# Two 3x3 convolutions of a basic block, four output rows at a time from six row combinations

## The chip, the cores and the metric

The kernel runs on one core of a Trainium2 chip. The metric is the device time of one execution in microseconds (us). All data is fp32. The engines are named as the profile names them: PE is TensorE (PEld its weight loads), DVE is VectorE, ACT is ScalarE, POOL is GpSimd, SP is SyncE, whose queue issues most DMAs. Each engine works through its own queue in order; semaphores order the engines among each other.

## What is computed

The input is a batch of 2 images with 128 channels of 128 x 128 points. Four layers follow each other: a convolution with a small state-space model on top, a density gate on windows, a second layer like the first, and a basic block. Only the last is touched by the change:

```python
def _L3_conv_ref(x, w1, gamma1, beta1, w2, gamma2, beta2):
    w1b = w1 + lax.stop_gradient(jnp.sign(w1) - w1)
    w2b = w2 + lax.stop_gradient(jnp.sign(w2) - w2)
    out = jax.nn.relu(_batchnorm(_conv3x3(x, w1b), gamma1, beta1))
    out = _batchnorm(_conv3x3(out, w2b), gamma2, beta2)
    out = out + x
    return jax.nn.relu(out)
```

Both convolutions have 128 input and 128 output channels, 3 x 3 taps and a border of zeros. The batch norms take mean and variance over both images, so a convolution must be complete before its norm can be applied. The input `x` of the block is itself the end of the second layer: silu of a normalised `y`, plus that layer's input.

## The kernel before, in words

`_program` runs the four layers one after the other. The basic block is `_basic_block` (line 820). Channels lie on the 128 partitions. An image is cut into bands of 8 rows (`BAND`), so there are 32 bands over both images, listed in `bands`. The result of a convolution stays in SBUF as `Y`, both images whole.

**Fewer products.** A convolution of 3 rows is not done tap by tap. For each pair of output rows, four combinations of four input rows are formed (`combine`, lines 874 to 881: row 0 minus row 2, row 1 plus row 2, row 2 minus row 1, row 1 minus row 3), the weights are combined in the same way beforehand (lines 838 to 853), and the four products are put together to two output rows. A band of 8 rows has 4 pairs, so each product is a matmul over 4 x 128 = 512 columns; with the three horizontal taps that is 12 matmuls a band in place of 18.

**Weights.** For each of the two weight sets the sign is taken on ACT (line 841), two DVE operations form w + (sign(w) - w) (lines 842 and 843), and DVE builds the four combined sets `u` (lines 848 to 852). The temporary tiles come from the buffers of `comb`, of which there are two.

**The loop.** `convolve` writes the order of every engine out by hand (`manual_schedule` for PE, ACT, DVE, POOL and SP): within it each engine's queue holds the instructions in exactly the order in which the Python code issues them. In round k it calls `load(k+3)`, the step `make(k+2)`, `combine(k+1)` and `conv(k)`:

- `load` (first convolution only): SP issues the DMAs of 10 rows of `y` (line 940) and of the residual `xs` (line 942).
- `make` is `residual` in the first convolution: ACT does the silu in place (line 948), POOL adds the residual (line 949), SP writes the rows to DRAM as `x3` (line 950). In the second it is `normalised`: POOL copies two rows from the band before (line 961), ACT applies norm and relu to rows of `Y` (line 963).
- `combine`: POOL, four instructions of 520 elements a partition (line 880), into a `comb` tile.
- `conv`: PE, 12 matmuls (line 887) into four banks of PSUM (tile `m`, two buffers); ACT copies one product to SBUF (line 895); DVE does four additions of 512 elements (lines 898 to 901), each with one operand in PSUM; two `bn_stats` (line 903).

Three tiles of 10 rows (`room`) hold the bands in turn. After a convolution `affine` (line 908) turns the statistics into scale and shift.

**The output stage** (lines 969 to 977) loads `x3` back, scales, adds, applies relu and stores; its tiles are in turn the two `xs` and the `comb` buffers.

Of the kernel before, what the change touches and what calls it, by code (L numbers as in the profile page):

```python
# [24 lines left out]
F32 = mybir.dt.float32  # L25
U8 = mybir.dt.uint8
AF = mybir.ActivationFunctionType
ALU = mybir.AluOpType
# [3 lines left out]
P = 128  # L32
# [10 lines left out]
BAND = 8  # L43
# [775 lines left out]

def _basic_block(tc, src, y, norm, x3, w1, w2, bn, out, B, H):  # L820

# [3 lines left out]
    nc = tc.nc  # L825
    pairs = BAND // 2
    with tc.tile_pool(name="bb", bufs=1) as cp, tc.tile_pool(name="bband", bufs=2) as bp, tc.tile_pool(
        name="ps_c", bufs=2, space=PSUM
    ) as pp:

        def combined():
            return bp.tile([P, 4, pairs, P + 2], F32, tag="comb", name="comb")

        bnc = cp.tile([P, 4], F32, tag="bnc", name="bnc")
        nc.sync.dma_start(out=bnc, in_=bn)
        ws = []
        for n, wd in enumerate((w1, w2)):
            room = [combined().rearrange("p a b c -> p (a b c)")[:, : 9 * P] for _ in range(2)]
            wt, sg = room
            nc.sync.dma_start(out=wt, in_=wd)  # L840
            nc.scalar.activation(sg, wt, AF.Sign)
            nc.vector.tensor_tensor(sg, sg, wt, ALU.subtract)
            nc.vector.tensor_tensor(wt, wt, sg, ALU.add)

            u = cp.tile([P, 4, 3, P], F32, tag=f"u{n}", name=f"u{n}")
            g = wt.rearrange("p (k t c) -> p k t c", k=3, t=3)
            half = sg.rearrange("p (k t c) -> p k t c", k=3, t=3)
            nc.vector.tensor_copy(u[:, 0:4:3], g[:, 0:3:2])
            nc.vector.tensor_tensor(half[:, 0], g[:, 0], g[:, 2], ALU.add)
            nc.vector.tensor_tensor(u[:, 1], half[:, 0], g[:, 1], ALU.add)  # L850
            nc.vector.tensor_tensor(u[:, 2], half[:, 0], g[:, 1], ALU.subtract)
            nc.vector.tensor_scalar_mul(u[:, 1:3], u[:, 1:3], 0.5)
            ws.append(u)
        Y = cp.tile([P, B, H, P], F32, tag="Y", name="Y")

# [17 lines left out]

        def combine(k):

            xb = span(k)[0]
            v = combined()
            d = [xb[:, n : n + BAND - 1 : 2, :] for n in range(4)]
            for i, (m, n, op) in enumerate(((0, 2, ALU.subtract), (1, 2, ALU.add), (2, 1, ALU.subtract), (1, 3, ALU.subtract))):
                nc.gpsimd.tensor_tensor(v[:, i], d[m], d[n], op)  # L880
            return v

        def conv(u, v, b, r0, stats):
            m = pp.tile([P, 4, pairs, P], F32, tag="m", name="m")
            for i in (1, 2, 0, 3):
                for kw in range(3):
                    nc.tensor.matmul(  # L887
                        m[:, i],
                        lhsT=u[:, i, kw, :],
                        rhs=v[:, i, :, kw : kw + P],  # L890
                        start=(kw == 0),
                        stop=(kw == 2),
                    )
            m1 = bp.tile([P, pairs, P], F32, tag="m1", name="m1")
            nc.scalar.copy(m1, m[:, 1])  # L895
            rows = Y[:, b, r0 : r0 + BAND, :]
            y0, y1 = rows[:, 0:BAND:2, :], rows[:, 1:BAND:2, :]
            nc.vector.tensor_tensor(y0, m1, m[:, 2], ALU.add)  # L898
            nc.vector.tensor_tensor(y1, m1, m[:, 2], ALU.subtract)
            nc.vector.tensor_tensor(y0, y0, m[:, 0], ALU.add)  # L900
            nc.vector.tensor_tensor(y1, y1, m[:, 3], ALU.subtract)
            for n in range(BAND // ROWS):
                nc.vector.bn_stats(
                    stats[:, (b * H + r0) // ROWS + n, :],
                    rows[:, n * ROWS : (n + 1) * ROWS, :].rearrange("p r w -> p (r w)"),
                )
# [9 lines left out]

        def convolve(u, load, make, n):

            stats = cp.tile([P, B * H // ROWS, 6], F32, tag="st", name="st")
            v = {}  # L920
            E = mybir.EngineType
            with tc.manual_schedule(engines={E.PE, E.Activation, E.DVE, E.Pool, E.SP}):
                for k in range(-3, len(bands)):
                    for ahead, f in ((3, load), (2, make)):
                        if 0 <= k + ahead < len(bands):
                            f(k + ahead)
                    if 0 <= k + 1 < len(bands):
                        v[k + 1] = combine(k + 1)
                    if k >= 0:
                        conv(u, v.pop(k), *bands[k], stats)  # L930
            return affine(stats, n)
# [19 lines left out]

        s1, t1 = convolve(ws[0], load, residual, 0)

# [12 lines left out]

        s2, t2 = convolve(ws[1], lambda k: None, normalised, 1)

# [12 lines left out]
def _program(ctx, tc, d, cols, out):  # L981
# [7 lines left out]
    with tc.tile_pool(name="const", bufs=1) as cp, tc.tile_pool(name="wts", bufs=1) as wp:  # L989
# [24 lines left out]
        with tc.tile_pool(name="ps_n", bufs=1, space=PSUM) as pp:  # L1014
            norm = [_norm(nc, npool, pp, w, con, stats, b) for b in range(B)]
    _basic_block(tc, x2, y, norm, x3, d["L3_w1"], d["L3_w2"], d["L3_bn"], out, B, H)

# [42 lines left out]
```

## Time and profile before

| quantity | us |
|---|---|
| median of 3 runs | 7720.45 |
| lowest, highest | 7717.87, 7742.86 |
| profiled execution, its own time | 7727.12 |
| span of the profiled execution | 7725.3 |
| basic block, first weight load to end | 6898.7 to 7725.3 |
| first convolution, first combination to last statistics | 6929.43 to 7268.34 |
| second convolution, the same | 7274.15 to 7612.91 |

The profile shows one execution. A page or an answer of it lists instructions by line, engine, operation and tile, as `out<-in`, with sizes as partitions x elements. In a timeline the first number is the start and the second the duration, both in us; what stands in brackets at the end is how long the engine had been idle before and what ended that. In the groups, `x1536 | 663.6, 595` means 1536 instructions, 663.6 us in which at least one of them ran, 595 ns the mean of one; then the idle time before them. TensorE's granted clock is given as a share of full speed.

### The profile page before, as it was taken

What the parts mean: (1) busy time and instruction counts of PE and PEld (TensorE: products, weight loads), DVE (VectorE), ACT (ScalarE), POOL (GpSimd) and SP (SyncE); (2) the same over time, 40 slices, a digit from 0 to 9 for tenths busy, and PEclk for the clock granted to TensorE, in tenths of its full rate; (3) what the DMA queues carried; (4) which work ended last, traced back from release to release, by engine and by line L of the source; (5) the groups of instructions that cost most, each with busy time, mean ns of one, the idle gap of its engine ahead of it and who ended that gap; (6) DMA issues with size and microseconds to landing.
All of it is one profiled execution on the core that took longest, in us unless ns stands there. A gap on an engine that the chain in (4) does not pass through costs nothing.

```text
span 7725.3 us, 87235 instructions
## 1 busy us (share of the span) xinstructions
PE 6471.5 (84%) x29648; PEld 2190.2 (28%) x29648; DVE 6761.0 (88%) x6304; ACT 4280.1 (55%) x4877; POOL 5630.1 (73%) x1879
## 2 busy tenths in 40 slices
PE   7888888888888888767888888888888888869993
PEld 2222222222222222243222222222222222224441
DVE  6999999999999999966999999999999999983333
ACT  5665666566666666554566656566666566631112
POOL 5777877887877778743787777787777887867541
PEclk8999999999999999877999999999999999979997
DMA  7999999999999999944999999999999999975204
GB/s 205 252 250 245 252 248 246 252 252 247 249 252 250 249 252 253 242 183 149 248 248 250 251 243 251 251 250 253 255 249 244 254 250 247 251 196 177 87 0 169
DMA packets 573438, 1767.29 MB, mean 229 GB/s; under 512 B 85536, under 2 KB 239680, under 8 KB 458176
## 3 DMA queue, kind: packets, MB, share of 16 engines
q1 hardware_dynamic: 568384, 1744.92, 86.4%
q10 hardware_dynamic: 4608, 16.78, 0.5%
q8 instruction: 236, 3.87, 0.2%
q14 instruction: 210, 1.72, 0.1%
HBM read 1551.65 MB, written 209.72 MB: 228 GB/s over the span
## 4 chain that ended last, share of the span: by engine, by line
DVE 37%; DMA 28%; PE 20%; issue 6%; ACT 4%; POOL 3%; SPq 2%; POOLq 0%; DVEq 0%; ACTq 0%
DMA bcr<-sb 21%; DVE set L472 12%; DVE h L477 11%; DVE r L473 10%; PE m L887 9%; DMA ur<-su 3%; POOL h L445 3%; PE set L454 2%; PE one L350 2%; ACT set L463 2%; PE ys L492 1%; PE one L400 1%; DVE v L505 1%; PE ys L483 1%; DMA sb<-bc 1%
## 5 line engine op out<-in xcount | busy, mean ns | idle before, releaser
L445 POOL TENSOR_TENSOR h<-ur,bcr 128x2048 f32<-128x2048 f32 x896 | 4060.8, 4539 | 1291.1 <-DMA bcr<-sb 1038.1
L472 DVE TENSOR_TENSOR set<-set,h 128x1024 f32<-128x1024 f32 x1792 | 2193.5, 1224 | 275.1 <-ACT set L463 170.4
L473 DVE TENSOR_TENSOR r<-set,bcr 128x1024 f32<-128x1024 f32 x1792 | 2194.5, 1225 | 61.5
L463 ACT ACTIVATE set<-set 128x1024 f32<-128x1024 f32 x1792 | 1745.2, 1006 | 844.2 <-PE set L454 833.2
L477 DVE TENSOR_TENSOR h<-set,h 128x1024 f32<-128x1024 f32 x1536 | 1865.9, 1215 | 25.0 <-POOL h L445 24.8
L454 PE MATMUL set<-dt,rep 32*128 32x512 f32 x7168 | 1396.1, 675 | 100.9 <-DVE h L477 94.8
L492 PE MATMUL ys<-r,ct 128*32 128x512 f32 x7168 | 1168.2, 635 | 32.7 <-DVE r L473 32.7
L323 PE MATMUL one<-band,conv 128*128 128x512 f32 x2304 | 1082.9, 606 | 22.6 <-DMA band<-in_x_dram 12.0
L400 PE MATMUL one<-xc,keep 128*64 128x512 f32 x1008 | 318.9, 715 | 462.9 <-ACT xc L357 355.7
L887 PE MATMUL m<-comb,u 128*128 128x512 f32 x1536 | 663.6, 595 | 39.0 <-POOL comb L880 39.0
L454 PEld LDWEIGHTS set<-dt,rep 32*128 32x128 f32 x7168 | 403.2, 193 | 992.5 <-issue 463.7
L323 PEld LDWEIGHTS one<-band,conv 128*128 128x128 f32 x2304 | 407.1, 189 | 669.1 <-issue 596.6
L483 PE MATMUL ys<-t,ct 128*128 128x512 f32 x512 | 327.9, 727 | 251.9 <-DVE v L505 250.3
L352 ACT ACTIVATE xc<-one,keep 128x512 f32<-128x512 f32 x252 | 173.3, 688 | 516.9 <-PE one L350 512.1
L492 PEld LDWEIGHTS ys<-r,ct 128*32 128x32 f32 x7168 | 180.9, 112 | 926.8 <-issue 764.3
L898 DVE TENSOR_TENSOR Y<-m,m 128x512 f32<-128x512 f32 x64 | 44.0, 688 | 435.8 <-ACT m L895 435.8
L880 POOL TENSOR_TENSOR comb<-band 128x520 f32<-128x520 f32 x256 | 298.5, 1198 | 161.7 <-PE m L887 160.1
L887 PEld LDWEIGHTS m<-comb,u 128*128 128x128 f32 x1536 | 291.7, 190 | 410.2 <-issue 363.3
L420 PE MATMUL one<-prod,ct 128*128 128x512 f32 x504 | 282.1, 642 | 118.0 <-POOL prod L412 89.9
L374 POOL TENSOR_TENSOR u<-dt,xc 128x1024 f32<-128x1024 f32 x128 | 303.0, 2367 | 89.7 <-ACT dt L368 89.3
L895 ACT COPY m<-m 128x512 f32<-128x512 f32 x64 | 37.5, 586 | 556.6 <-issue 474.7
L350 PE MATMUL one<-y,w_in 128*128 128x512 f32 x504 | 344.2, 772 | 1.8 <-ACT xc L352 1.8
(144 smaller groups left out, 6292.1 us busy)
## 6 DMA issues: line engine op xcount, KB each, us to landing
ur<-su SPq DMA_DIRECT2D x896, 896.0 KB, 11.6
bcr<-sb SPq DMA_DIRECT2D x896, 448.0 KB, 11.8
ur<-su SPq DMA_DIRECT2D x896, 128.0 KB, 11.2
su<-u SPq DMA_DIRECT2D x1024, 64.0 KB, 3.1
sb<-bc SPq DMA_DIRECT2D x256, 224.0 KB, 2.7
bcr<-sb SPq DMA_DIRECT2D x896, 64.0 KB, 11.1
y<-o SPq DMA_DIRECT2D x128, 256.0 KB, 9.4
band<-in_x_dram SPq DMA_DIRECT2D x28, 640.0 KB, 10.9
```

Source lines behind the costliest of these rows:

```text
L323: nc.tensor.matmul(py.rearrange("p (r w) -> p r w", r=ROWS), lhsT=w["conv"][:, tap, :], rhs=xb[:, r + kh : r + kh + ROWS, kw : kw + P], st ...
L350: nc.tensor.matmul(p, lhsT=w[("in", "z")[i]][:, g, :], rhs=s["y"], start=True, stop=True)
L400: nc.tensor.matmul(p[g * NQ * DS : (g + 1) * NQ * DS, :], lhsT=w[("xb", "xcm")[i]], rhs=s["xc"][:, g, :], start=True, stop=True,)
L445: nc.gpsimd.tensor_tensor(b, s["ur", t], s["bc", t][:, 0].unsqueeze(1).to_broadcast([P, NJ, NS]), ALU.mult)
L454: nc.tensor.matmul(a[j // 2][:, j % 2, :], lhsT=w["rep"][r, q, :], rhs=s["dt"][r, g, :], start=True, stop=True, tile_position=(r.start, 0),)
L463: nc.scalar.activation(x, x, AF.Exp)
L472: nc.vector.tensor_tensor(pt, pt, s["h", t - 1][:, js, :], ALU.mult)
L473: nc.vector.tensor_tensor(s["r", t][:, js, :], pt, s["bc", t - 1][:, 1].unsqueeze(1).to_broadcast([P, 2, NS]), ALU.mult)
L477: nc.vector.tensor_tensor(s["h", t][:, js, :], pt, s["h", t][:, js, :], ALU.add)
L483: nc.tensor.matmul(s["ys", g], lhsT=con["ident"], rhs=s["t1"][:, g, :], start=True, stop=False)
L492: nc.tensor.matmul(s["ys", g][a : a + NQ * DJ, :], lhsT=red[:, q, :], rhs=r[:, j, :], start=False, stop=(q == NQ - 1), tile_position=(0, a),)
L887: nc.tensor.matmul(m[:, i], lhsT=u[:, i, kw, :], rhs=v[:, i, :, kw : kw + P], start=(kw == 0), stop=(kw == 2),)
```

## The change

The convolutions are done four output rows at a time from six combinations of six input rows, with weights combined accordingly. Of a band of 8 rows there are now two groups of four (`fours`), so each product has 2 x 128 = 256 columns, and there are six products of three taps: 18 matmuls of 256 columns a band.

The combinations have factors other than 1 and are made in two pieces: `edges` (four DVE `scalar_tensor_tensor` of 260 elements and three POOL `tensor_tensor` of 520, 520 and 260) and `rest_of` (three more DVE operations of 260, in place). `products` is the matmuls alone; `m` takes three banks and keeps two buffers. `conv` copies one bank of two products to SBUF (`c`), forms sums and differences of the products, those of one pair in SBUF (`sd1`) and those of the other in PSUM (`sd2`), and writes `Y` with five more operations.

The pieces of a band are issued one to four rounds apart: in round k, `rest_of(k+1)`, `products(k)`, `conv(k-1)`, `load(k+4)`, `make(k+3)`, `edges(k+2)`. `comb` has three buffers of 6 x 2 x 130 elements in place of two of 4 x 4 x 130.

The six weight sets take more room, so there is one `u`. The second convolution's weights are prepared at the start in a part of `Y` that isn't in use yet, stored to DRAM (`later`) and loaded into `u` between the convolutions.

```diff
         def combined():
-            return bp.tile([P, 4, pairs, P + 2], F32, tag="comb", name="comb")
+            return bp.tile([P, 6, fours, P + 2], F32, tag="comb", name="comb", bufs=3)
...
+            nc.vector.tensor_scalar_mul(x[:, 0], g[:, 0], 0.25)
+            nc.vector.tensor_copy(x[:, 5], g[:, 2])
+            nc.vector.tensor_tensor(even, g[:, 0], g[:, 2], ALU.add)
+            nc.vector.tensor_tensor(x[:, 3], even, g[:, 1], ALU.add)
+            nc.vector.tensor_tensor(x[:, 2], even, g[:, 1], ALU.subtract)
+            nc.vector.tensor_scalar_mul(x[:, 2:4], x[:, 2:4], -1.0 / 6.0)
+            flat = [y.rearrange("p t c -> p (t c)") for y in (even, odd, g[:, 0], g[:, 1], g[:, 2], x[:, 1], x[:, 4])]
+            nc.vector.scalar_tensor_tensor(flat[0], flat[4], 4.0, flat[2], ALU.mult, ALU.add)
+            nc.vector.scalar_tensor_tensor(flat[5], flat[3], 2.0, flat[0], ALU.mult, ALU.add)
+            nc.vector.scalar_tensor_tensor(flat[6], flat[3], -2.0, flat[0], ALU.mult, ALU.add)
+            nc.vector.tensor_scalar_mul(x[:, 1:5:3], x[:, 1:5:3], 1.0 / 24.0)
+        later = scratch.tile([P, 18 * P], F32, tag="later", name="later", bufs=1)
+        nc.sync.dma_start(out=later, in_=spare.rearrange("p a t c -> p (a t c)"))
...
-        def combine(k):
+        def edges(k):
 
             xb = span(k)[0]
             v = combined()
-            d = [xb[:, n : n + BAND - 1 : 2, :] for n in range(4)]
-            for i, (m, n, op) in enumerate(((0, 2, ALU.subtract), (1, 2, ALU.add), (2, 1, ALU.subtract), (1, 3, ALU.subtract))):
-                nc.gpsimd.tensor_tensor(v[:, i], d[m], d[n], op)
+            low, high = [xb[:, n : n + BAND, :].rearrange("p (i n) w -> p n i w", n=4) for n in (0, 2)]
+            for n, at in enumerate((0, 3, 2, 5)):
+                nc.vector.scalar_tensor_tensor(v[:, at], low[:, n], -4.0, high[:, n], ALU.mult, ALU.add)
+            nc.gpsimd.tensor_tensor(v[:, 1:5:3], high[:, 1:3], low[:, 1:3], ALU.subtract)
+            nc.gpsimd.tensor_tensor(v[:, 0:6:5], v[:, 2:6:3], v[:, 0:4:3], ALU.subtract)
+            nc.gpsimd.tensor_tensor(v[:, 3], v[:, 2], v[:, 3], ALU.add)
             return v
 
-        def conv(u, v, b, r0, stats):
-            m = pp.tile([P, 4, pairs, P], F32, tag="m", name="m")
-            for i in (1, 2, 0, 3):
+        def rest_of(v):
+            x = [v[:, n].rearrange("p i w -> p (i w)") for n in range(6)]
+            nc.vector.scalar_tensor_tensor(x[4], x[1], -2.0, x[4], ALU.mult, ALU.add)
+            nc.vector.scalar_tensor_tensor(x[1], x[1], 4.0, x[4], ALU.mult, ALU.add)
+            nc.vector.scalar_tensor_tensor(x[2], x[2], 2.0, x[3], ALU.mult, ALU.subtract)
+
+        def products(v):
+
+            m = pp.tile([P, 3, 2, fours, P], F32, tag="m", name="m")
+            for n, i in enumerate((2, 4, 3, 1, 0, 5)):
                 for kw in range(3):
                     nc.tensor.matmul(
-                        m[:, i],
+                        m[:, n // 2, n % 2],
...
+            return m
+
+        def conv(m, b, r0, stats):
+            c = bp.tile([P, 2, fours, P], F32, tag="c", name="c")
+            nc.scalar.copy(c, m[:, 0])
+            sd1 = bp.tile([P, 2, fours, P], F32, tag="sd", name="sd", bufs=1)
+            sd2 = pp.tile([P, 2, fours, P], F32, tag="sd", name="sd")
+            for n, sd in enumerate((sd1, sd2)):
+                nc.vector.tensor_tensor(sd[:, 0], m[:, 1, n], c[:, n], ALU.add)
+                nc.vector.tensor_tensor(sd[:, 1], m[:, 1, n], c[:, n], ALU.subtract)
             rows = Y[:, b, r0 : r0 + BAND, :]
-            y0, y1 = rows[:, 0:BAND:2, :], rows[:, 1:BAND:2, :]
-            nc.vector.tensor_tensor(y0, m1, m[:, 2], ALU.add)
-            nc.vector.tensor_tensor(y1, m1, m[:, 2], ALU.subtract)
-            nc.vector.tensor_tensor(y0, y0, m[:, 0], ALU.add)
-            nc.vector.tensor_tensor(y1, y1, m[:, 3], ALU.subtract)
+            y = rows.rearrange("p (i n) w -> p n i w", n=4)
+            (s1, d1), (s2, d2) = [(sd[:, 0], sd[:, 1]) for sd in (sd1, sd2)]
+            nc.vector.tensor_tensor(y[:, 0:4:3], m[:, 2], sd1, ALU.add)
+            nc.vector.scalar_tensor_tensor(y[:, 1], d2, 2.0, d1, ALU.mult, ALU.add)
+            nc.vector.scalar_tensor_tensor(y[:, 2], s2, 4.0, s1, ALU.mult, ALU.add)
+            nc.vector.tensor_tensor(y[:, 0], s2, y[:, 0], ALU.add)
+            nc.vector.scalar_tensor_tensor(y[:, 3], d2, 8.0, y[:, 3], ALU.mult, ALU.add)
...
-                for k in range(-3, len(bands)):
-                    for ahead, f in ((3, load), (2, make)):
+                m = {}
+                for k in range(-4, len(bands) + 1):
+                    if 0 <= k + 1 < len(bands):
+                        rest_of(v[k + 1])
+                    if 0 <= k < len(bands):
+                        m[k] = products(v.pop(k))
+                    if k >= 1:
+                        conv(m.pop(k - 1), *bands[k - 1], stats)
+                    for ahead, f in ((4, load), (3, make)):
                         if 0 <= k + ahead < len(bands):
                             f(k + ahead)
-                    if 0 <= k + 1 < len(bands):
-                        v[k + 1] = combine(k + 1)
-                    if k >= 0:
-                        conv(u, v.pop(k), *bands[k], stats)
+                    if 0 <= k + 2 < len(bands):
+                        v[k + 2] = edges(k + 2)
...
+        nc.sync.dma_start(out=u.rearrange("p a t c -> p (a t c)"), in_=later)
+        s2, t2 = convolve(lambda k: None, normalised, 1)
```

## The prediction

> **What bounds the kernel now.** I read first the chain of work that ended last: inside the basic block it is one piece per convolution, TensorE line 887 from 6932.1 to 7263.9 us and again from 7276.6 to 7608.4. Then the busy time by stretch:
>
> ```profile
> 6942.00:7263.00 321.00, 321.00 (x749) 141.37 (x748) 116.80 (x186) 57.10 (x60) 216.10 (x153) 1.00 0.52 164
> 7287.00:7608.00 321.00, 321.00 (x749) 141.18 (x747) 116.77 (x186) 51.13 (x60) 149.69 (x150) 1.00 0.01 2
> ```
>
> Columns after the length: busy us of PE, weight loads, DVE, ACT, POOL, then clock, DMA share, GB/s. TensorE has no idle time at full clock; DVE works 36%, POOL 67% and 47%. So TensorE sets both convolutions. The groups from 6800 us on give prices:
>
> ```profile
> L887 PE MATMUL m<-comb,u 128*128 128x512 f32 x1536 | 663.6, 595 | 39.0 <-POOL comb L880 39.0
> L880 POOL TENSOR_TENSOR comb<-band 128x520 f32<-128x520 f32 x256 | 298.5, 1198 | 161.7 <-PE m L887 160.1 <-DVE u L851 1.6
> ...
> L975 DVE SCALAR_TENSOR_TENSOR comb<-Y,aff_s,comb 128x1024 f32<-128x1024 f32 x16 | 20.5, 1284 | 39.2 <-DMA comb<-x 39.0
> ```
>
> Each fp32 matmul is two records (1536 = 64 bands x 12 x 2). One band in the timeline:
>
> ```profile
> 7150.61 0.59 ACT L895 COPY m<-m 128x512 f32<-128x512 f32 x1 [8.36 <-issue]
> 7151.09 1.46 ACT L948 ACTIVATE band<-band,aff_t,aff_s 128x1280 f32<-128x1280 f32 x1
> 7151.23 0.69 DVE L898 TENSOR_TENSOR Y<-m,m 128x512 f32<-128x512 f32 x1 [6.50 <-ACT m L895]
> 7151.84 0.68 DVE L899 TENSOR_TENSOR Y<-m,m 128x512 f32<-128x512 f32 x1
> 7152.43 0.68 DVE L900 TENSOR_TENSOR Y<-Y,m 128x512 f32<-128x512 f32 x1
> 7152.63 2.68 POOL L949 TENSOR_TENSOR band<-band,xs 128x1280 f32<-128x1280 f32 x1 [3.01 <-ACT band L948]
> 7153.03 0.68 DVE L901 TENSOR_TENSOR Y<-Y,m 128x512 f32<-128x512 f32 x1
> 7153.75 1.29 DVE L903 BATCH_NORM_STATS2 st<-Y 128x6 f32<-128x512 f32 x2
> 7155.27 4.65 POOL L880 TENSOR_TENSOR comb<-band 128x520 f32<-128x520 f32 x4
> ```
>
> The next L895 is at 7160.91: a band lasts 10.30 us. DVE operations of 512 elements start 0.60 apart though each lasts 0.68, except that bn_stats waits for L901's end (0.72). L880 starts every 1.16.
>
> Last, what no steady band shows: DVE operations with two SBUF inputs beside POOL. The weight preparation has them:
>
> ```profile
> 6920.76 2.71 POOL L949 TENSOR_TENSOR band<-band,xs 128x1152 f32<-128x1152 f32 x1 [8.95 <-DMA xs<-x]
> 6921.26 3.43 DVE L843 TENSOR_TENSOR comb<-comb 128x1152 f32<-128x1152 f32 x1
> ...
> 6924.78 3.03 POOL L949 TENSOR_TENSOR band<-band,xs 128x1280 f32<-128x1280 f32 x1 [1.31 <-DMA xs<-x]
> 6925.19 3.03 DVE L849 TENSOR_TENSOR comb<-comb 128x384 f32<-128x384 f32 x1
> ```
>
> Alone, these DVE lines took 1.34 and 0.56 us (first weight set). Here each stood until POOL's instruction ended (6923.47, 6927.81), then ran: ends 1.22 and 0.41 later. And after line 660, with two POOL instructions back to back:
>
> ```profile
> 3509.68 4.68 POOL L662 TENSOR_TENSOR x<-xr,g 128x1024 f32<-128x1024 f32 x2 [4.46 <-ACT g L660]
> 3511.61 0.52 DVE L760 TENSOR_SCALAR e<-e 128x128 f32<-128x128 f32 x1
> 3513.16 1.28 DVE L762 TENSOR_SCALAR e<-e 128x128 f32<-128x128 f32 x1
> ```
>
> L760 got through where the first L662 ended (3512.0); it did not wait for the second. A DVE operation already standing slips between two POOL instructions; one that comes after the second has begun waits it out (L762).
>
> **What the Trainium skill says.** "SBUF — State Buffer", Who interferes with whom: a Vector instruction with two SBUF inputs and a GpSimd instruction that reads SBUF exclude each other for a whole instruction; with one SBUF input it does not contend. The rows above agree, and L898 to L901 (one input in PSUM) keep 0.68 beside L949. "TensorE: Matmul & The Clock Gate", Step-by-step: the next weights load under the running matmul. Agrees: 0.19 us loads under matmuls 0.429 apart. The same page, Part 1: some 3.4 us of idleness halve the clock. After the 12.7 us pause at 7264 the first matmuls stood 0.85 apart for 4 us.
>
> **The change, part by part (per band).**
> TensorE: 18 matmuls of 256 columns for 12 of 512. 24 records in 10.30 us are 0.429 each; half the columns is 0.215, above the 0.19 of a load (line 512 runs 16 records of 128 columns, with loads, in 2.05, 0.13 each). 36 x 0.215 = 7.75 us. Gain alone: 2.55 x 64 = 163 us, if nothing else is late.
>
> DVE: now 4 operations and 2 statistics; then 18. Slope 1.05 ns an element (L842, 1152: 1.36; L849, 384: 0.56), so start to start 256 elements cost 0.60 - 256 x 1.05 = 0.33, 260 cost 0.34. A scalar_tensor_tensor with immediate scalars isn't in the trace; L975, with per-partition scalars, starts every 1.20 against 1.14 for a tensor_tensor of 1024: 0 to 0.065 more; I take 0.03. Names: R1 to R3 are rest_of, S1 to S4 the sums and differences, W1 to W5 the writes to Y, E1 to E4 the edges; P1 to P3 POOL's three in edges.
> S1 to the next edges: S 4 x 0.33 + W1 0.60 + W2 to W4 3 x 0.33 + 0.06 + W5 to its end 0.48 + two statistics 1.21 = 4.7. None has two SBUF inputs (sd2 and m are PSUM).
> E1 to the end of E4: 3 x 0.37 + 0.44 = 1.55.
> Then the place that decides. Order on DVE: E(k+2), at once R(k+1) of the next round, whose operands came from the E and P just before. From E4's end = 0: R1 starts at -0.08 and holds the port to 0.34; P2 (520 elements, needs E4) runs to 1.54; R2 slips in to 1.84; P3 (260; 1.16 - 260 x 2.1 ns = 0.61) to 2.4. R3 needs P3's result. POOL's queue has its next instruction waiting: in the first convolution residual's L949 (operands ready for us: the load is issued a round earlier and lands in 4.5 to 5.6), which begins before R3 has its signal. R3 stands 2.69 to 5.1, and S1 starts at 5.3. In the second the next is L961, 0.40: S1 at 3.0.
> Behind the waiting R3 on DVE stand conv's nine operations, the statistics and the next edges; TensorE waits for R3 (its first product reads that combination) and for W1, which frees m. Nothing else may run in DVE's queue meanwhile.
> load and make move one round further ahead and behind conv: on ACT the copy of m now precedes the silu (both done a round early); on POOL the order residual, then combinations stays; on SP the three DMAs of a band (4.5, 5.6 and 3.2 us to landing) keep their order and have the whole longer round: nothing, and if a load came late, L949 would move behind R3, a gain.
> So a round is 5.3 + 4.7 + 1.55 = **11.55 us** in the first convolution and 3.0 + 4.7 + 1.55 = **9.25** in the second. TensorE's 7.75 (9.8 if 4 us of each round ran at half clock after the 3.8 us pause) lies under both, m being double; ACT (0.59 + 1.46), POOL (5.6) and the DMAs (1.8 MB a round) too. DVE, not TensorE, sets the end.
> Whole convolutions, E1(0) to the last statistics: 1.55 + two rounds without conv + 29 full + (R and conv) + two conv alone. First: 1.55 + 13.7 + 335 + 10 + 9.4 = 370, against 6929.43 to 7268.34 = 339 now: **+31**. Second: 1.55 + 9.1 + 268 + 7.7 + 9.4 = 296 against 7274.15 to 7612.91 = 339: **-43**.
> Setup: some 5 more DVE operations for each weight set, 2.3 us each; the second set no longer waits for a buffer (its load was issued at 6912.45, now with the first). I take +1; -3 to +10, the high end if the store of the second set holds the band loads behind it on SP's queue. The reload of u (1.18 MB; some 8 us from 4.5 for 0.64 MB) starts at the last matmul and is wanted after conv's rest, 5.8 us of affine and normalising, E and R, some 13 us: nothing; uncovered, it would cost 8. The output stage keeps its chain (xs slots): 0, bounds -3 and +3.
> Sum: +31 - 43 + 1 = -11. On the profiled 7727.1 (span 7725.3): 7716; the median is 6.7 lower, so **7709**.
>
> **Rivals.**
> *R3 gets ahead of L949*, if POOL needs a moment to start it: S1 at 2.75 in the first convolution, 2.55 x 32 = 82 less: 7627. For: L760 slipped in. Against: it stood there already, and consecutive L880 overlap by 0.04.
> *No exclusion for this operation*: S1 at 2.25 in both; 3.05 x 32 + 0.75 x 32 = 122 less: 7587. Against: L843, L849.
> *Slower: DVE loses every hand-over.* R2 stands behind P2, P3, the residual or copy and P1 of the next band: S1 at 6.5 and 4.2, 1.2 x 64 = 77 more: 7786. For: POOL's queue is full there. Against: L760. It decides once the two rounds add up to over 21.1 us (I have 20.8): 0.3 us is all that lies between.
>
> **How the numbers follow.** The likeliest case has 0.52; its ends come from the scalar_tensor_tensor price (10 x 0.03 x 62 = 19 down, 10 x 0.035 x 62 = 22 up), setup and output: 7685 to 7744. R3 ahead 0.13, no exclusion 0.06, lost hand-overs 0.20, smaller waits on DVE not counted here (some 7750) 0.09. Range 7625 to 7790: only the 7587 and tails lie outside. A measurement tells 0.3%, 23 us, from no change. Faster: 0.19 + a third of the likeliest case = 0.35; same: the bulk of it = 0.33; slower: 0.29 + the rest = 0.32.
>
> **What would show it.** TensorE idle in every round, records of 256 columns 0.215 apart; rounds of 11.5 and 9.25 us; R3 lasting about 2.9 us in the first convolution and starting just after L949 begins; R2 about 1.5; S and W at 0.33. Wrong if R3 is short, if the rounds of both convolutions are alike, or if TensorE is still without idle time.

## The result, and the profile after

| | before | after |
|---|---|---|
| median of 6 runs each, us | 7726.12 | 7682.67 |
| lowest, highest | 7716.18, 7742.86 | 7668.24, 7699.44 |
| profiled execution, its span | 7725.3 | 7676.1 |

The ratio after to before is 0.9943, 95% interval 0.9924 to 0.9962: 0.57% faster, some 43 us.

The totals also hold the three layers ahead of the basic block, which no kernel here touches. In thirteen profiled executions, one of each kernel of this study, they ended between 6883 and 6923 us. So from here on stages inside the block are compared. Setup runs from the first weight load to the first combination on DVE (on POOL in the kernel before), a convolution from there to its last statistics; the block is the sum of all stages with the 5 to 6 us of affine and normalising between the convolutions.

| stage, us | before | after | difference | predicted |
|---|---|---|---|---|
| setup | 30.7 | 25.6 | -5.1 | +1 |
| first convolution | 338.9 | 360.7 | +21.8 | +31 |
| second convolution | 338.8 | 295.6 | -43.1 | -43 |
| output stage | 112.4 | 101.4 | -11.0 | 0 |
| block | 826.6 | 788.7 | -37.9 | -11 |

Of the two profiled executions' 49 us, 11 lie ahead of the block (6898.75 against 6887.43) and are not the change's. The cut between setup and first convolution is soft: in the kernel after and six of its variants the two from the first weight load to the first R3 (named below) take 33.8 us, while the setup alone varies from 23.1 to 26.7.

The windows of the kernel after, in the middle of each convolution (columns: busy us and number of PE, weight loads, DVE, ACT, POOL; then clock, DMA share, GB/s):

```profile
6950.00:7230.00 280.00, 220.33 (x906) 182.30 (x904) 261.70 (x456) 48.76 (x51) 158.65 (x104) 0.93 0.52 166
7300.00:7530.00 230.00, 208.45 (x943) 176.18 (x942) 211.21 (x458) 44.91 (x52) 101.65 (x103) 1.00 0.00 1
```

Before, PE filled such windows wholly. Now it is busy 79% and 91%, and DVE 93% and 92%: DVE has taken its place. The groups of the kernel after, from 6880 us on:

```profile
L906 PE MATMUL m<-comb,u 128*128 128x256 f32 x2304 | 537.4, 394 | 137.3 <-DVE Y L926 90.8 <-DVE comb L899 46.5
L899 DVE SCALAR_TENSOR_TENSOR comb<-comb 128x260 f32<-128x260 f32 x64 | 97.4, 1521 | 39.5 <-POOL comb L892 39.5
L898 DVE SCALAR_TENSOR_TENSOR comb<-comb 128x260 f32<-128x260 f32 x64 | 88.8, 1388 | 2.2
L897 DVE SCALAR_TENSOR_TENSOR comb<-comb 128x260 f32<-128x260 f32 x64 | 28.0, 438 | 5.0 <-POOL comb L890 5.0
```

PE waited 137 us, all of it for DVE: 46.5 for the first combination of each convolution, 90.8 in the rounds. Three DVE operations of the same form and size, R1 to R3 (lines 897 to 899), took 438, 1388 and 1521 ns on average. A longer operation that has no more to compute is one that stood. One round of the first convolution, in the timeline:

```profile
7100.44 0.42 DVE L897 SCALAR_TENSOR_TENSOR comb<-comb 128x260 f32<-128x260 f32 x1
7100.60 1.42 POOL L891 TENSOR_TENSOR comb<-comb 128x520 f32<-128x520 f32 x1 [4.97 <-DVE comb L889]
7100.90 1.41 DVE L898 SCALAR_TENSOR_TENSOR comb<-comb 128x260 f32<-128x260 f32 x1
7102.09 0.80 POOL L892 TENSOR_TENSOR comb<-comb 128x260 f32<-128x260 f32 x1
7102.85 2.68 POOL L983 TENSOR_TENSOR band<-band,xs 128x1280 f32<-128x1280 f32 x1
7102.93 2.89 DVE L899 SCALAR_TENSOR_TENSOR comb<-comb 128x260 f32<-128x260 f32 x1 [0.63 <-POOL comb L892]
...
7108.02 9.70 PE L906 MATMUL m<-comb,u 128*128 128x256 f32 x36 [3.34 <-DVE Y L926]
```

R2 stands behind P2 (line 891) and gets through where P2 ends, ahead of P3 (line 892). R3 needs P3's result and starts 0.08 us after the residual (line 983); it ends 0.29 after the residual has. The next R3 starts at 7114.27: a round of 11.34 us. The second convolution:

```profile
7412.57 0.40 POOL L995 COPY band<-band 128x256 f32<-128x256 f32 x1
7412.66 0.59 DVE L899 SCALAR_TENSOR_TENSOR comb<-comb 128x260 f32<-128x260 f32 x1 [0.63 <-POOL comb L892]
```

The instruction behind P3 is now the copy of two rows, 0.40 us, and R3 lasts 0.59. Rounds are 9.04 us.

### The profile page after: what moved, and what is told of

Same layout as the page of the kernel before. It is cut to its first block, busy times and chain, and to the rows that moved or that the text cites. A ratio compares the mean times of both kernels' runs of the same rounds, so it can differ in the third digit from the quotient of the medians.

```text
span 7676.1 us, 89472 instructions
## 1 busy us (share of the span) xinstructions
PE 6354.0 (83%) x30416; PEld 2345.8 (31%) x30416; DVE 7120.0 (93%) x7082; ACT 4278.8 (56%) x4877; POOL 5563.7 (72%) x1815
## 4 chain that ended last, share of the span: by engine, by line
DVE 49%; DMA 22%; PE 12%; issue 7%; ACT 4%; POOL 4%; SPq 1%; POOLq 0%; DVEq 0%; ACTq 0%
DMA bcr<-sb 16%; DVE set L472 15%; DVE h L477 13%; DVE r L473 12%; DMA ur<-su 3%; PE set L454 2%; PE one L350 2%; POOL h L445 2%; ACT set L463 2%; PE one L400 2%; PE ys L492 1%; DVE v L505 1%; DVE comb L899 1%; PE ys L483 1%; POOL comb L891 1%
## 5 line engine op out<-in xcount | busy, mean ns | idle before, releaser
L472 DVE TENSOR_TENSOR set<-set,h 128x1024 f32<-128x1024 f32 x1792 | 2192.9, 1224 | 263.5 <-ACT set L463 161.8
L906 PE MATMUL m<-comb,u 128*128 128x256 f32 x2304 | 537.4, 394 | 137.3 <-DVE Y L926 90.8
L906 PEld LDWEIGHTS m<-comb,u 128*128 128x128 f32 x2304 | 449.8, 197 | 224.6 <-issue 100.3
L917 ACT COPY c<-m 128x512 f32<-128x512 f32 x64 | 37.5, 586 | 517.9 <-PE m L906 292.2
L364 PE MATMUL one<-xc,w_dt 128*128 128x512 f32 x504 | 312.1, 704 | 2.7 <-ACT bc L407 2.7
```

What stands on the lines that cost most here:

```text
L472: nc.vector.tensor_tensor(pt, pt, s["h", t - 1][:, js, :], ALU.mult)
L906: nc.tensor.matmul(m[:, n // 2, n % 2], lhsT=u[:, i, kw, :], rhs=v[:, i, :, kw : kw + P], start=(kw == 0), stop=(kw == 2),)
```

## The experiments

**Theory (port):** rounds are set by DVE operations with two SBUF inputs that stand behind POOL instructions; what counts is which of the two has begun first. **Rival (loop):** the ring of dependences from combinations to products to sums sets the round, and the standing R3 only fills time in which DVE would wait anyhow.

**e1: conv ahead of rest_of in DVE's queue.** Only the place of one call in `convolve` changes; since `rest_of` has DVE operations alone, no other engine's order does.

```diff
-                    if 0 <= k + 1 < len(bands):
-                        rest_of(v[k + 1])
                     if 0 <= k < len(bands):
                         m[k] = products(v.pop(k))
                     if k >= 1:
                         conv(m.pop(k - 1), *bands[k - 1], stats)
+                    if 0 <= k + 1 < len(bands):
+                        rest_of(v[k + 1])
```

> DVE's order in a round becomes conv(k-1), rest_of(k+1), edges(k+2); nothing else moves. Theory port (in the changed kernel R2 and R3 of rest_of stand behind POOL's two-input instructions, which hold the SBUF port; DVE sets the round): the two subtractions of edges and the residual now run beside conv, which has no operation with two SBUF inputs, so R1 to R3 find POOL nearly done. A round is about 8.2 us in the first convolution (4.6 conv, up to 1 us behind POOL's last instruction, 1.1 R, 1.4 E) and in the second TensorE's own 7.75. First convolution about 270 us (361 now), second about 258 (296 now): some 125 us less, near 7558 us. Theory loop (TensorE's products wait for the m buffer that W1 frees, and this loop through PSUM, slowed by the half clock after each pause, sets the round of 11.3 us, with R3 only filling the time): the loop W1, products, W1 is as long as before, so rounds stay at 11.3 and 9.0 us and the time stays near 7683 us.

Measured: 7602.73 us (4 runs; before beside it 7737.78), ratio 0.9815, 0.9791 to 0.9839. First convolution 283.9, second 263.0. The residual now runs beside conv's operations, which have at most one SBUF input. Timeline of this kernel in the first convolution:

```profile
7096.48 2.69 POOL L983 TENSOR_TENSOR band<-band,xs 128x1280 f32<-128x1280 f32 x1
...
7098.98 0.48 DVE L897 SCALAR_TENSOR_TENSOR comb<-comb 128x260 f32<-128x260 f32 x1
7099.12 1.49 POOL L890 TENSOR_TENSOR comb<-band 128x520 f32<-128x520 f32 x1
...
7099.49 1.40 DVE L898 SCALAR_TENSOR_TENSOR comb<-comb 128x260 f32<-128x260 f32 x1
7100.81 0.42 DVE L899 SCALAR_TENSOR_TENSOR comb<-comb 128x260 f32<-128x260 f32 x1
```

R3 takes 0.42. R2 still stands, behind P1 (line 890) of the next band; that keeps the round at 8.25 us instead of TensorE's 7.77, much as expected. The stage missed the expected 270 because its filling and emptying had been put too low: 25.5 us lie ahead of the first R3 and behind the last, and one of the first rounds took 12.9. The same operations in another order take 77 us off the first convolution: the loop theory falls.

**e2: the residual between P1 and P2.** The last two POOL operations of `edges` become a function `differences`, called after `make`:

```diff
-                    for ahead, f in ((4, load), (3, make)):
-                        if 0 <= k + ahead < len(bands):
-                            f(k + ahead)
+                    if 0 <= k + 4 < len(bands):
+                        load(k + 4)
                     if 0 <= k + 2 < len(bands):
                         v[k + 2] = edges(k + 2)
+                    if 0 <= k + 3 < len(bands):
+                        make(k + 3)
+                    if 0 <= k + 2 < len(bands):
+                        differences(v[k + 2])
```

> POOL's order only: first edges instruction, then the residual, then the two subtractions, so that what follows the second subtraction in POOL's queue is the next band's first edges instruction (520 elements, 1.2 us) in place of the residual (2.7 us). Theory port: R3 stands about 1.5 us in place of 2.9, the round of the first convolution is about 9.9 us (11.34 now), the first convolution about 320 us (361 now); the second unchanged (its R3 stands behind 1.2 us in place of 0.4: round 9.8, about 24 us more). Theory loop: both rounds unchanged, 11.3 and 9.0 us.

Measured (one run, as for all below unless said): 7697.89 us; first convolution 324.1, second 321.5; rounds 9.95 in both. The timeline of this kernel:

```profile
7100.37 1.28 POOL L890 TENSOR_TENSOR comb<-band 128x520 f32<-128x520 f32 x1
7100.45 1.49 DVE L901 SCALAR_TENSOR_TENSOR comb<-comb 128x260 f32<-128x260 f32 x1 [0.63 <-POOL comb L895]
7101.61 2.87 POOL L988 TENSOR_TENSOR band<-band,xs 128x1280 f32<-128x1280 f32 x1
```

What stands behind P3 is now P1 in both convolutions, 1.28 us, and R3 takes 1.49 in both: 37 us less in the first, 26 more in the second. R3's duration follows the instruction behind P3, whichever that is. It gets in where P1 ends, and the residual lasts 0.2 longer (2.87 instead of 2.68).

**e3: the residual in two halves.** `half = (hi - lo) // 2`, and `r` is the popped tile:

```diff
-            nc.gpsimd.tensor_tensor(x, x, rests.pop(k), ALU.add)
+            nc.gpsimd.tensor_tensor(x[:, :half], x[:, :half], r[:, :half], ALU.add)
+            nc.gpsimd.tensor_tensor(x[:, half:], x[:, half:], r[:, half:], ALU.add)
```

> The residual is added in two POOL instructions of 640 elements, same place in the queue. Theory port: a DVE operation that already stands gets the port between two POOL instructions, so R3 waits for the first half only, about 1.5 us in place of 2.9: round of the first convolution 10.0 us (11.34 now), about 40 us less in the first convolution, second unchanged. If DVE had to wait until POOL's queue is empty, or under theory loop: no change within 3 us.

Measured: 7674.6 us; first convolution 330.7, second 296.0; round 10.11. The timeline of this kernel:

```profile
7101.76 1.44 POOL L985 TENSOR_TENSOR band<-band,xs 128x640 f32<-128x640 f32 x1
7101.83 1.66 DVE L899 SCALAR_TENSOR_TENSOR comb<-comb 128x260 f32<-128x260 f32 x1 [0.63 <-POOL comb L892]
7103.17 1.59 POOL L986 TENSOR_TENSOR band<-band,xs 128x640 f32<-128x640 f32 x1
```

The same sum in two instructions costs POOL more (3.0 us instead of 2.68) and takes 30 us off the first convolution, where about 40 had been expected: R3, already standing, goes between the halves.

**e4: R3 with one input in PSUM.** `p` is a part of the last `sd2`; the third combination is therefore not the reference's. The line that matters:

```diff
-            nc.vector.scalar_tensor_tensor(x[2], x[2], 2.0, x[3], ALU.mult, ALU.subtract)
+            nc.vector.scalar_tensor_tensor(x[2], x[3], 2.0, p, ALU.mult, ALU.subtract)
```

> R3 takes its second operand from PSUM (an older tile of sums) and its first from the tile that POOL has just written, so it still waits for POOL's result but has one SBUF input; the third combination is therefore not the reference's. Theory port: R3 lasts 0.43 us although the residual runs beside it; round of the first convolution 8.9 us (11.34 now), of the second 8.9 (9.04 now); first convolution about 285 us (361 now). Theory loop, or a wait that has nothing to do with the number of SBUF inputs: R3 may be short, but the rounds stay at 11.3 and 9.0 us.

Measured: 7638.67 us; first convolution 300.9, second 289.3; round 8.88. The timeline of this kernel:

```profile
7106.26 2.67 POOL L989 TENSOR_TENSOR band<-band,xs 128x1280 f32<-128x1280 f32 x1
7106.33 0.42 DVE L902 SCALAR_TENSOR_TENSOR comb<-comb,sd 128x260 f32<-128x260 f32 x1 [0.62 <-POOL comb L892]
```

The order and the starting times are those of the kernel after (0.07 behind the residual), and R3 takes 0.42. So it is the two SBUF inputs, not the queue or the semaphore, that make it stand. The Trainium skill, "SBUF — State Buffer", Who interferes with whom, says that a DVE operation with at most one SBUF input doesn't contend with POOL, outside what it calls the 2-port perf modes; this pair of rows agrees. The rounds are what was expected; the stage came out 16 above it, because the time ahead of the first R3 and behind the last, 27 us beside the 273.8 between them, had been put too low.

**e5: the second pair of sums in SBUF.**

```diff
-            sd2 = pp.tile([P, 2, fours, P], F32, tag="sd", name="sd")
+            sd2 = bp.tile([P, 2, fours, P], F32, tag="sd2", name="sd2", bufs=1)
```

> The kernel after, with the second pair of sums and differences (sd2) in SBUF instead of PSUM, so that W2 to W5 each have two or three SBUF operands. Theory (a DVE operation with two SBUF inputs stands behind a POOL instruction that runs): in this order POOL has nothing to run between P1 of the next band, about 1.5 us after R3, and P2, which waits for E4; W2 to W5 fall into that gap, so the convolutions stay within 3 us of 360.7 and 295.7 us. Rival (the sums in PSUM are what makes this kernel's second convolution short): the second convolution gets longer by 0.3 us or more in a round, 10 to 45 us in all.

Measured: 7691.59 us; first convolution 363.9, second 291.0. In the order of the kernel after, PSUM for these sums buys nothing: the second convolution is 4.6 us shorter without it (rounds 8.92 instead of 9.04), a little more than the theory allowed, since the two operations that write sd2 start 0.33 apart instead of 0.45. In the first, the stage is 3.2 longer, but 2.5 of that lie ahead of the first R3, and the setup is 2.5 shorter. The rounds are 11.22 instead of 11.34, except at three image borders, where they take 10.2 to 10.4 instead of 8.9. In these R3 gets ahead of the residual (see e9), and then the residual does run beside the W operations. The timeline of this kernel in one of them:

```profile
7066.88 2.89 POOL L983 TENSOR_TENSOR band<-band,xs 128x1280 f32<-128x1280 f32 x1
7069.07 0.98 DVE L927 SCALAR_TENSOR_TENSOR Y<-sd,sd 128x256 f32<-128x256 f32 x1
7069.72 1.48 POOL L890 TENSOR_TENSOR comb<-band 128x520 f32<-128x520 f32 x1
7069.98 1.51 DVE L928 SCALAR_TENSOR_TENSOR Y<-sd,sd 128x256 f32<-128x256 f32 x1
```

W2 stands until the residual ends and W3 behind P1; in the other rounds both take 0.41.

**e7: the same edit on the kernel of e1**, where POOL works while W2 to W5 run.

> The kernel with conv ahead of rest_of on DVE, with the second pair of sums and differences in SBUF. There POOL runs P3, the residual and P1 while W2 to W5 run. Theory: two of W2 to W5 stand behind the residual (2.7 us) and P1 (1.4 us), and R2 no longer stands behind P1 (1.0 back): round of the first convolution 8.24 + 3.1 = about 11.3, the stage 283.9 to some 375; second convolution, where the copy of 0.4 stands in the residual's place, 8.2 to 8.7 a round and 275 to 292 in all instead of 263.1. Rival (keeping the sums in PSUM is worth nothing; only the order of R3 and the residual counts): 284 and 263, W2 to W5 at 0.42 each.

Measured: 7659.54 us; first convolution 357.5, second 283.5; rounds 10.86 and 8.58. The timeline of this kernel:

```profile
7110.84 2.86 POOL L983 TENSOR_TENSOR band<-band,xs 128x1280 f32<-128x1280 f32 x1
7111.09 2.90 DVE L928 SCALAR_TENSOR_TENSOR Y<-sd,sd 128x256 f32<-128x256 f32 x1
7113.66 1.47 POOL L890 TENSOR_TENSOR comb<-band 128x520 f32<-128x520 f32 x1
7113.91 1.51 DVE L929 TENSOR_TENSOR Y<-sd,Y 128x256 f32<-128x256 f32 x1
```

Two of the W operations stand, as expected: W3 behind the residual and W4 behind P1; R2 no longer does. The first convolution is 17 us below the expected 375, since a round is 10.86 and not 11.3. Here the sums in PSUM are worth 74 and 20 us. Which operands go to PSUM matters only beside POOL's work.

**e6: the kernel before with three buffers for the combinations** (`bufs=3` in `combined`'s tile; nothing else).

> The kernel before, with three buffers for the combinations instead of two and nothing else changed. Theory (the output stage of the kernel after was 11 us shorter because the third buffer lets one more load of x3 be under way): output stage 101 to 104 us instead of 112.4, both convolutions unchanged at 339. Setup a few us shorter, since the second set's load no longer waits for a buffer (25 to 28 instead of 30.7). Rival (the output stage differs because the end of the convolution leaves the queues or the clock in another state): output stage stays at 111 to 113.

Measured: 7696.32 us; convolutions 339.1 and 339.0, setup 26.6, output stage 100.9 instead of 112.4. The output stage takes its tiles from `xs` and `comb` in turn. The group of waits, first for the kernel before and then for this one:

```profile
L975 DVE SCALAR_TENSOR_TENSOR comb<-Y,aff_s,comb 128x1024 f32<-128x1024 f32 x16 | 20.5, 1284 | 39.2 <-DMA comb<-x 39.0
```

```profile
L975 DVE SCALAR_TENSOR_TENSOR comb<-Y,aff_s,comb 128x1024 f32<-128x1024 f32 x16 | 20.4, 1284 | 31.1 <-DMA comb<-x 28.8 <-ACT comb L976 2.3
```

Waits for the loads into `comb` fall by 10 us. The third buffer alone accounts for the output stage (11.6 of 11.0) and can account for the setup (4.1 of 5.1); neither needs four rows at a time. All kernels with three buffers had an output stage of 100.5 to 105.1 and a setup of 23.1 to 27.6.

**e9: one more POOL instruction.** In three rounds of the kernel after, at image borders, R3 did not stand. Its timeline there:

```profile
7051.32 0.20 POOL L881 MEMSET band<- 128x130 f32 x1
7051.41 0.43 DVE L899 SCALAR_TENSOR_TENSOR comb<-comb 128x260 f32<-128x260 f32 x1 [0.63 <-POOL comb L892]
7051.49 2.90 POOL L983 TENSOR_TENSOR band<-band,xs 128x1280 f32<-128x1280 f32 x1
```

A memset of the border lay between P3 and the residual. So a memset that nobody needs was put there in every round (`pad` has 130 elements a partition):

```diff
             nc.gpsimd.tensor_tensor(v[:, 3], v[:, 2], v[:, 3], ALU.add)
+            nc.gpsimd.memset(pad, 0.0)
             return v
```

> The kernel after, with one more POOL instruction at the end of edges, behind P3: a memset of a tile of 130 elements a partition that nothing reads. Theory (what makes R3 stand is that the instruction behind P3 in POOL's queue has begun before P3's result is signalled to DVE, 0.08 us before R3): the memset takes that place, holds POOL for some 0.2 us, and R3 gets its operands' port ahead of the residual, as in the three rounds of the kernel after in which a border's memset stood there (R3 0.43, round 8.88). So R3 0.43 in all rounds, 8.9 a round in the first convolution and 8.88 instead of 9.03 in the second: stages of some 285 to 295 instead of 360.7 and 291 instead of 295.7, total some 70 less. Rival (R3 loses to whatever POOL has queued, because POOL as a whole goes first): R3 2.7 to 3.1, rounds 11.4 and 9.2, some 3 to 6 us more in each convolution.

Measured: 7639.88 us (4 runs; before beside it 7730.88), ratio 0.9888, 0.9866 to 0.9910. First convolution 300.6, second 290.0; rounds 8.88 in both. The timeline of this kernel:

```profile
7125.58 0.20 POOL L894 MEMSET pad<- 128x130 f32 x1
7125.66 0.43 DVE L901 SCALAR_TENSOR_TENSOR comb<-comb 128x260 f32<-128x260 f32 x1 [0.62 <-POOL comb L893]
7125.74 2.88 POOL L985 TENSOR_TENSOR band<-band,xs 128x1280 f32<-128x1280 f32 x1
```

A useless instruction takes 60 us off the first convolution and 6 off the second (70 in all expected). In one of the first rounds DVE reaches R3 late, 0.09 us after the residual has begun, and R3 still stands (2.90). R3 starts while the memset runs and does not stand for it (the same section of the skill says that only a POOL instruction which reads SBUF excludes it); the residual begins 0.08 later and is the one that stands, 2.88.

**e10: the same memset with one element a partition.**

> The same with a memset of one element a partition. Theory: it decides by how long POOL is held. If the memset holds POOL for more than 0.08 us (R3 began 0.08 after the residual), the result is that of the longer memset, rounds of 8.8 and 8.8; if it is shorter, R3 stands behind the residual as before, 11.34 and 9.04. I expect the first, since the shortest operations of POOL in the trace take some 0.06 to 0.2 us each.

Measured: 7693.34 us; first convolution 364.2, second 295.8; rounds 11.38 and 9.08. The timeline of this kernel:

```profile
7126.35 0.09 POOL L894 MEMSET pad<- 128x1 f32 x1
7126.40 2.66 POOL L985 TENSOR_TENSOR band<-band,xs 128x1280 f32<-128x1280 f32 x1
7126.43 2.92 DVE L901 SCALAR_TENSOR_TENSOR comb<-comb 128x260 f32<-128x260 f32 x1 [0.63 <-POOL pad L894]
```

I had expected this memset to be long enough; it was not. (The shortest POOL instructions of the kernel after last 0.10 us, not 0.06; but what counts is when the next one starts, and its three memsets of 20 elements, line 868, start 0.05 apart.) It holds POOL for 0.05 us, R3 comes 0.03 after the residual, and stands all of it. Of the 3.5 us by which the first convolution is longer than in the kernel after, 2.5 are again the setup's. 0.05 is too little, 0.16 is enough: the point at which the round changes by 2.5 us lies between, where the 0.08 of the kernel after is.

**e11: P3 moved from POOL to DVE** in the kernel of e1, as one more operation of `rest_of`:

```diff
-            nc.gpsimd.tensor_tensor(v[:, 3], v[:, 2], v[:, 3], ALU.add)
...
+            nc.vector.tensor_tensor(x[3], x[2], x[3], ALU.add)
             nc.vector.scalar_tensor_tensor(x[2], x[2], 2.0, x[3], ALU.mult, ALU.subtract)
```

> The kernel with conv ahead of rest_of on DVE, with P3 moved from POOL to DVE (one of the three edits of the best version so far, alone). Theory (POOL's time plus the time of the DVE operations with two SBUF inputs makes the round): P2 1.29 + residual 2.68 + P1 1.4 + four R 1.35 + E 1.43 = 8.15, against 8.24 with P3 on POOL; so 8.1 to 8.2 a round and 280 to 284 for the first convolution, and the rest of the way to 269.9 belongs to the copied rows. Rival (the copied rows are worth nothing, P3 alone freed it): 7.8 a round, 270.

Measured: 7591.5 us; first convolution 282.7, rounds 8.17. As the port theory counts it: 0.08 less a round although DVE has an operation more. R1 now stands for 0.9 us behind P1, in R2's place.

**e8: the best version.** To e11 it adds that ACT copies the two rows which a band shares with the one before, so that silu, residual and loads are done for 8 rows (`load` is shortened in the same way), and that the store of the second weight set follows the fourth load:

```diff
+            if lo == 0:
+                nc.scalar.copy(xb[:, 0:2, 1 : P + 1], span(k - 1)[0][:, BAND : BAND + 2, 1 : P + 1])
+                lo = 2
             x = xb[:, lo:hi, 1 : P + 1]
             nc.scalar.activation(x, x, AF.Silu, bias=norm[b][1], scale=norm[b][0])
```

> The kernel with conv ahead of rest_of on DVE, with less of POOL's time in the first convolution: the two rows that a band shares with the one before it are copied by ACT instead of computed again (residual 1024 elements instead of 1280, 2.15 us instead of 2.68), P3 moved from POOL to DVE as one more operation of rest_of (0.34 instead of 0.74), and the store of the second set of weights issued behind the fourth load. Theory (port): POOL's P2 + residual + P1 = 1.29 + 2.15 + 1.45 = 4.9, then R 1.35 and E 1.43 make 7.7, just under TensorE's 7.76; so both convolutions are bound by TensorE, 7.76 to 7.85 a round, the first 264 to 270 us instead of 283.9, the second 263. Setup 20 to 23 instead of 23.2 if the store held the loads, 23 to 24 if not. Total some 15 to 20 below the kernel with conv first, about 7585. Rival (DVE's own count of operations decides): one more operation on DVE makes 8.24 + 0.34 = 8.6 a round, the first convolution 294.

Measured: 7558.67 us (5 runs, 7547.74 to 7573.27; before beside it 7721.19), ratio 0.9787, 0.9764 to 0.9810. First convolution 269.9, second 263.5. Of the 13 us less than in e11, 10 are the shorter rounds behind the third R3, the copied rows' part; 2.5 lie ahead of it, where the place of the store and the smaller loads change together. The setup is 23.1, as in e1 and e11, so the place of the store makes no difference to that. The windows of this kernel:

```profile
6990.00:7170.00 180.00, 180.00 (x835) 157.72 (x835) 176.82 (x442) 46.30 (x68) 108.89 (x73) 1.00 0.63 201
7230.00:7430.00 200.00, 200.00 (x928) 175.26 (x927) 195.94 (x490) 43.98 (x51) 74.77 (x79) 1.00 0.00 1
```

PE has no idle time in either, at full clock, in rounds of 7.77 us, though DVE is busy 98% too. This version beats both kernels: the two convolutions take 144 us less than before, of the 163 that fewer products alone were put at; the rest lies in filling and emptying the pipeline.

## Why the prediction was right, and where it was off

The path and who stands where came out as predicted; the size of the gain did not. 7682.67 lies in the range, but two below the likeliest case's 7685 to 7744, and the block is 38 us shorter where 11 were forecast.

**TensorE no longer sets the end: right.** Records of the kernel after follow each other every 0.216 us where PE is kept busy (e1: 7.77 for the 36 of a round; 0.215 predicted). In the first convolution PE paused 14 times for 3.06 to 3.34 us. After 11 of these pauses a round's 36 records took 9.67 to 10.77 us, after three, of 3.32 and 3.33 us, the usual 8.01; the mean clock in the window was 0.93. The Trainium skill, "TensorE: Matmul & The Clock Gate", Part 1, puts the slow clock behind an idle window of some 3.4 us; here pauses as short as 3.06 were followed by it, and the length alone doesn't tell which are. It cost nothing, since DVE sets the round; the prediction had 9.8 for it.

**Who stands behind whom: right.** R1 through, R2 behind P2 and into the gap ahead of P3, R3 behind the residual or the copy. From E4's end (7100.52 in the round shown) R2 was predicted to end at 1.84 and S1 to start at 5.3; measured 1.79 and 5.22. e2 to e4, e9 and e10 change in turn the instruction behind P3, its length, R3's operands and the start of the residual, and R3's duration follows each. The rival in which R3 gets ahead of the residual (7627) did happen, in the three rounds with a border's memset; made to happen in all, it gave 7640 (e9).

One reading behind the prediction was wrong, without harm to the sum. The prediction listed L760 and L762 among the operations with two SBUF inputs, and took the rows to agree that one SBUF input doesn't contend. Both are tensor_scalar operations with one input, and both stood. The kernel after has another, first alone and then behind a residual:

```profile
6899.61 0.36 DVE L851 TENSOR_SCALAR u<-comb 128x384 f32<-128x384 f32 x1
...
6907.29 2.40 POOL L983 TENSOR_TENSOR band<-band,xs 128x1152 f32<-128x1152 f32 x1 [6.84 <-ACT band L982]
6907.37 2.54 DVE L851 TENSOR_SCALAR Y<-comb 128x384 f32<-128x384 f32 x1
```

So not every operation with one SBUF input goes free; conv's, which read PSUM beside it, do. The section cited at e4 excepts its 2-port perf modes; whether these operations ran in one, no run here shows.

**Second convolution: 296 predicted, 295.6 measured**, but that it agrees so closely is luck. From the third R3 to the last there are 29 rounds in 263 us, 9.07 each, not 9.25: 5 less. The filling and the emptying of the pipeline took 3 and 2 more, which happens to make up for it.

**First convolution: +31 predicted, +21.8 measured.** The terms that were off:

- The round was 11.34, not 11.55. The mis-sized term is the price of a scalar_tensor_tensor with immediate scalars: "0 to 0.065 more; I take 0.03". E1 to E4 and R and W start 0.33 to 0.34 apart, as a tensor_tensor does; the extra is 0. That also shortens "E1 to the end of E4" from 1.55 to 1.43; S1 comes 0.08 earlier. 23 such rounds: 5 us.
- Three rounds with a border's memset were 8.88. The prediction had the memsets of `border` nowhere in POOL's order: 8 us.
- Two rounds have a residual of 1152 elements (11.07 and 11.10), and one of the last has no residual left and P1 in its place (9.95, R3 1.50); the prediction counted all as full: 3 us.
- The other way, the start: R3 of the third band came 25.0 us after E1(0), not 17.9, because the P1 it needs is queued on POOL behind band 3's residual, whose silu waited for its load until 6928.59: 7 us more. That load was issued at 6919.79, right behind the store of the second weight set (6918.88), and so took up to 8.8 us where the prediction has 4.5. In e8, with the store behind it (and 8 rows in place of 10), the silu began 4.2 us after the issue. The risk that the prediction named for the setup came true here; that the store is the cause is likely, not shown alone.

**Setup and output stage: wrong.** "The output stage keeps its chain (xs slots): 0, bounds -3 and +3" failed. I had seen that `comb` buffers went from two to three, and used it for the setup's loads only; but the output stage draws from the same pool, and the prediction's own row for L975 showed 39 us of waiting for just those loads. e6 shows it: 112.4 to 100.9 with nothing else changed. In the setup the same buffer let the second weight load go early, 3.8 us behind the first instead of 13.7; e6 has 4.1 less with nothing else changed. "I take +1" had counted the added operations and not what the earlier load takes off.

So of the 27 us by which the block came out shorter than the sum, 11 are the output stage, 9 the first convolution and 6 the setup. The range held, and the gain itself was small for the reason given: TensorE gained some 82 us in each convolution, and DVE gave back all of it and 22 more in the first and 38 of it in the second, as time spent standing behind POOL or waiting for it.

**Keeping the sums of one pair of products in PSUM** gains nothing where it was put (e5), because in that order POOL has nothing to run while W2 to W5 do, except in three border rounds. It is worth 94 us in the order of e1 (e7).

## What to carry to other kernels

When work moves from POOL and PE to DVE, count for each DVE operation with two SBUF inputs (in this kernel also for a tensor_scalar with one) what POOL has begun at that moment, not how busy either engine is; order the queues so that POOL's long instructions run beside DVE's operations that read PSUM. Where a DVE operation needs a POOL result, look at what stands behind that result in POOL's queue: here, where it was ready, it began first. And when a pool of buffers grows for one stage, look for every other stage that draws from it.

## What the runs showed that I had not expected

- The hand-over is decided by less than 0.1 us. R3 0.03 to 0.08 us behind a residual stands for 2.9; 0.08 ahead of it, the residual takes 2.88 to 2.90 instead of 2.68 and R3 0.43. A useless memset of 0.20 us on POOL is worth 2.46 us a round.
- A DVE operation that already stands gets in between two POOL instructions that follow each other at once (R2 in every round, R3 between the residual's halves at 1.66), and the POOL instruction behind it takes up to 0.2 us longer.
- The two DVE operations that write sd2 start 0.45 us apart when it lies in PSUM and 0.33 when it lies in SBUF (e5).
- The upstream layers vary by up to 40 us between executions, as much as the whole effect: the two profiled spans differ by 49 us, the blocks in them by 38.
